# A conv block on one core: other places for every operation, and a depthwise chain whose taps are placed over 1.86 jobs instead of one

## The chip, the cores and the metric

The kernel runs on one core of one Trainium2 chip. The metric is the device time of one execution in microseconds (us). Five engines of the core matter: TensorE (PE in the profile, with its weight loads as PEld), VectorE (DVE), ScalarE (ACT), GpSimd (POOL) and SyncE (SP). Each works off its own list of instructions in the order in which the program holds them; an instruction that is not ready holds up everything behind it on its engine. SP and POOL also issue the DMA transfers.

## The reference

The input x has the shape (16, 128, 96, 96): 16 images, 128 channels, 96 rows of 96 pixels, all in float32. One layer is computed:

```python
x_hwc = x.transpose(0, 2, 3, 1)
xn1 = _layernorm(x_hwc, ln1_w, ln1_b)                      # over the 128 channels
x = x + _attention(xn1, wq, wk, wv, wp).transpose(0, 3, 1, 2)   # 8 heads, channels attend to channels
xn2 = _layernorm(x.transpose(0, 2, 3, 1), ln2_w, ln2_b).transpose(0, 3, 1, 2)
# _ffn, with HID = 512:
h1 = jnp.einsum('bchw,oc->bohw', xn2, w_in[:, :, 0, 0])    # 128 -> 512 channels
h2 = depthwise 3x3 conv of h1 with w_dw, padding 1          # 512 channels, each for itself
h3 = jax.nn.gelu(h2, approximate=False)
x = x + jnp.einsum('bchw,oc->bohw', h3, w_out[:, :, 0, 0])  # 512 -> 128 channels
```

The attention matrices are 16 x 16 per head, made from sums over all 9216 pixels of an image. So the first norm (called a) has to run over a whole image before its attention is known; then comes the second norm (b), band by band, and the feed-forward part behind it.

## The kernel before

Channels lie on the 128 partitions. An image is cut into 8 bands of 12 rows (`BR`), a band into 3 units of 4 rows (`UR`, 384 pixels). The 512 hidden channels are 4 chunks of 128. A **job** is one band of one chunk: the hidden product on TensorE (`hidden`, L906), its copy from PSUM into one of four h1 buffers, one for each chunk (`kept`, L911, ScalarE), the nine taps of the depthwise conv, and the gelu (L944, ScalarE). There are 451 jobs, and not 512, because for some bands (`by_pe`) the conv of the fourth chunk is done wholly on TensorE, with weights that hold the tap (`comp`, L990).

The nine taps of an ordinary job are shared out in this way. The weights are scaled so that the centre tap has the factor 1. Two taps (three in one kind of job) are made by ScalarE as whole products into `pr` buffers (`products`, L919); POOL issues DMA transfers that add them, one into another (`add_last`, pr<-pr) and the sum into h3 (`add_first`, h<-pr; both L940). The five or six taps that are left are the **chain** on VectorE: the first one (L924) reads two windows of h1 and writes h3, and each later one (L930) multiplies a window of h1 by a column and adds h3 to it, in place. So each instruction of a chain needs the result of the one before it in that chain. The gelu needs h3 after the chain and after `add_first`. After it `out` (L1017, TensorE) sums four chunks per unit, and `add` (L1024, VectorE) adds that to x; SP stores the band.

Norm a and norm b run through transposes on TensorE (`forth`, L614), statistics on VectorE (`stats`, L621), two small instructions on POOL for the reciprocal root (`variance` and `power`, L628 and L632), for norm b a tiny shift on VectorE (`shift`, L636), a scaling on ScalarE (L668 and L672), transposes back (`back`, L719) and a copy into the padded xn buffers (`place`, L723 and L725). While band after band of one image goes through norm b and the feed-forward part, norm a of the next image is spread between.

**What sets the order.** No order is written out by hand. Every operation is recorded in a plan with its engine, an assumed duration, what it reads and writes, and a *place*: a number counted in jobs. A constant of its kind, from the table `AT`, is added to the number of the job (kinds that end in `_0` hold for the first image):

```python
    def at(kind, place, i=1):
        return place + AT[kind if i else kind + "_0"]
...
        for k, t in enumerate(left):
            dve(t_dve(tap_size(t)), at("tap", j + STEP["tap"] * k), lambda t=t: tap(t), h1, h3, True)
```

`Plan.order` then goes through an assumed course of the work: whenever an engine is free, it takes, of the operations whose needs are met and whose buffers are free, the one with the lowest place. A place is thus no time but a priority, compared with others on the same engine alone; a result counts as there only some hundred nanoseconds after its operation. For VectorE this means that the next instruction of a chain isn't ready in the moment in which its predecessor ends (`own`, 120 ns in the plan), and an instruction of another kind or of another chain is taken first if one is ready. For the buffers `tr`, `h3`, `pr`, `xb` and `x1` the order of the places is binding too (`IN_TURN`). The program then holds the operations of every engine in the order of their assumed starts. `AT`, at L37, and `STEP`, at L47, are all that the change touches; its table takes one line more, so that every line behind it has a number higher by one in the changed kernel.

Of the kernel before, what the change touches and what calls it, by code (L numbers as in the profile page):

```python
# [34 lines left out]
X1_BUFS, XB_BUFS, PR_BUFS, H3_BUFS, ZT_BUFS = 2, 6, 5, 10, 3  # L35
IN_TURN = ("tr", "h3", "pr", "xb", "x1")
AT = dict(  # L37
    load_w=-20.2, weights=13.4, zeros=-68.05, load_a=-147.85, forth_a=-13.65, stats_a=-60.15, variance_a=574.05,
    power_a=353.05, scaled_a=35.3, gram=0.3, back_a=-44.8, place_a=177.6, attention=-146.15, mix=-16.25,
    residual=204, mixed=-47.8, add_x=-331.2, forth_b=-11.5, stats_b=-104.75, variance_b=68.55, power_b=-326.9,  # L40
    shift_b=-87.05, scaled_b=162.15, back_b=-5.95, place_b=38.15, halo=227.9, hidden=2.75, kept=-114.4,
    products=153.15, add_last=-10.05, tap=4.7, add_first=-147.85, gelu=241.95, conv=3.5, conv_gelu=5.8, out=7,
    add=-70.85, store=278.2, mix_0=-75.3, residual_0=369.55, mixed_0=-142.3, add_x_0=-398.7, gram_0=126.2,
    forth_a_0=-269.2, forth_b_0=-14.9, stats_a_0=-113.85, stats_b_0=-48.05, scaled_a_0=100.95, scaled_b_0=286.6,
    back_a_0=-115.65, back_b_0=-181.55, place_a_0=-352.8, place_b_0=-9.75, shift_b_0=-101.75, late=-3.55,
)
STEP = dict(scaled=0.3, hidden=0.1, products=0.5, tap=0.166, conv=1.6, conv_tap=0.03, out=0.8, out_part=0.05)  # L47
SLACK = 300
NORM1_END = 6.0
EARLY = 5  # L50
# [162 lines left out]
def tile_restormer_block(  # L213
# [148 lines left out]
    def at(kind, place, i=1):  # L362
        return place + AT[kind if i else kind + "_0"]
# [5 lines left out]
    def z_units(k, r0, r1):  # L369

        return [("z", k, u) for u in range((r0 + UR - 1) // UR - 1, (r1 - 2) // UR + 1)]


    def t_mm(n):
        return 2 * max(111, 0.849 * n)

    def t_dve(n):
        return 100 + 1.067 * n if n > 2 * UT else 67 + 1.05 * n

    def t_act(n, scalars=0):  # L380
        return 95 + 93 * scalars + 0.832 * n
# [4 lines left out]
    def pe(ns, p, f, r, w):  # L386
        op("PE", ns, p, f, r, w, ns + 200 + SLACK, ns)

    def dve(ns, p, f, r, w, two=False):
        op("DVE", ns, p, f, r, w, ns + 120 + SLACK, ns + 120, two=two)  # L390
# [7 lines left out]
    def act(ns, p, f, r, w):  # L398
        op("ACT", ns, p, f, r, w, ns + 150 + SLACK, ns + 150)
# [155 lines left out]
    def norm(i, second, place_of):  # L555
# [41 lines left out]
        def pixels(s, m):  # L597
# [99 lines left out]
            for h, (q, tr) in enumerate(zip(qs, trs)):  # L697
                zt, sh = zt_of(q), s + STEP["scaled"] * h
                if by_dve:
# [8 lines left out]
        def zt_of(q):  # L708
            return ("h3", ("zT", q // 2), q % 2) if i == 0 and not second else ("zT", (name, q))
# [176 lines left out]
    def conv_job(j, g, n):  # L886
# [30 lines left out]
        def product(t):  # L917
            to = d["pr", t] = prp.tile([P, BR, W], F32, tag="pr", name=f"pr_{g}_{n}_{t}")
            nc.scalar.activation(to, shifted(t), AF.Copy, scale=ratio[:, n, t : t + 1])  # L919

        def tap(t):
            h3 = h3_of(g, n)
            if t == left[0]:
                nc.vector.scalar_tensor_tensor(  # L924
                    h3, shifted(t), ratio[:, n, t : t + 1], shifted(UNIT), ALU.mult, ALU.add
                )
                return
            lo, hi, cut = inside(t, b * BR, BR)
            to = h3[:, lo:hi, cut]
            nc.vector.scalar_tensor_tensor(  # L930
                to, shifted(t)[:, lo:hi, cut], ratio[:, n, t : t + 1], to, ALU.mult, ALU.add
            )

        def tap_size(t):
            lo, hi, cut = inside(t, b * BR, BR)
            return BR * W if t == left[0] else (hi - lo) * (cut.stop - cut.start)
# [16 lines left out]
        for k, (r, e) in enumerate(chunks):  # L953
            ph = ("h", (jn, r))
            jk, zs = j + STEP["hidden"] * k, z_units(kz, r0 + r, r0 + e)
            to = h1[k + 1 : k + 2] if r > 1 else h1[:2]
            pe(t_mm((e - r) * W), at("hidden", jk), lambda r=r, e=e: hidden(r, e), [*zs, ("w", "in")], [ph])
            act(t_copy((e - r) * W), at("kept", jk), lambda r=r, e=e: kept(r, e), [ph], to)
        for k, t in enumerate(dma_taps):
            jk = j + STEP["products"] * k  # L960
            act(t_act(BR * W, 1), at("products", jk), lambda t=t: product(t), h1, [("pr", (jn, t))])
# [3 lines left out]
        for k, t in enumerate(left):  # L965
            dve(t_dve(tap_size(t)), at("tap", j + STEP["tap"] * k), lambda t=t: tap(t), h1, h3, True)
        if dma_taps:
# [7 lines left out]
    def by_matmuls(p, g, s):  # L975
# [9 lines left out]
        def product(t):  # L985
            if t == order[0]:
                d["pc"] = rows(bank((g, PE_CHUNK, s), UT))
            lo, hi, cut = inside(t, b * BR + s * UR, UR)
            dy, dx = divmod(t, 3)
            nc.tensor.matmul(  # L990
                d["pc"][:, lo:hi, cut], lhsT=comp[:, t, :], rhs=window(xn, r0 + dy, UR, dx)[:, lo:hi, cut],
                start=(t == order[0]), stop=(t == order[-1]),
            )

        def columns(t):
            lo, hi, cut = inside(t, b * BR + s * UR, UR)
            return (hi - lo) * (cut.stop - cut.start)
# [4 lines left out]
        for k, t in enumerate(order):  # L1002
            dy = t // 3
            zs = z_units(kz, r0 + dy, r0 + dy + UR)
            pe(t_mm(columns(t)), at("conv", p + STEP["conv_tap"] * k), lambda t=t: product(t), [*zs, ("w", "conv")], [pc])
        act(t_act(UT), at("conv_gelu", p), gelu, [pc], [("h3", (g, PE_CHUNK), s)])

    def ffn_out(p, g, s):
# [5 lines left out]
        def product(k, n):  # L1014
            if k == 0:
                d["po"] = bank(("out", g, s), UT)
            nc.tensor.matmul(  # L1017
                rows(d["po"]), lhsT=woutT[:, n, :], rhs=h3s[g, n][:, s * UR : (s + 1) * UR, :],
                start=(k == 0), stop=(k == NCH - 1),
            )  # L1020
# [9 lines left out]
        for k, n in enumerate(order):  # L1030
            pk = p + STEP["out_part"] * k
            pe(t_mm(UT), at("out", pk), lambda k=k, n=n: product(k, n), [("h3", (g, n), s), ("w", "out")], [po])
# [69 lines left out]
```

## Time and profile before

| what | value |
|---|---|
| median of 3 runs (lowest to highest) | 4140.04 us (4127.82 to 4140.15) |
| the profiled execution's own time | 4139.28 us |
| its span in the trace | 4137.5 us |
| granted TensorE clock, mean over the span | 0.997 |
| TensorE busy, share of the span | 4064.3 us, 98% |
| VectorE busy | 4048.7 us, 98% |
| ScalarE busy | 3674.7 us, 89% |
| POOL busy | 2538.1 us, 61% |
| VectorE's chain instructions (L924 and L930) | 451 + 2129, together 3524.7 us |
| DMA adds issued by POOL (L940) | 578 + 450 of 576 KB each |

A row of a group has the line, the engine, the operation, what is written and read, the shapes and the count; then the busy time of the whole group and the mean duration of one instruction; then how long the engine had been idle just before instructions of the group, and what ended most of that. On VectorE an instruction's record reaches a little into that of the next one, so the cost of an instruction is better read as the distance from its start to the next start.

### The profile page before, as it was taken

To read this page: it belongs to the slowest core of one execution; us is meant where nothing else is said; L and a number is where in the kernel's file an instruction comes from. 1 tells how busy PE (TensorE), PEld (TensorE's weight loads), DVE (VectorE), ACT (ScalarE), POOL (GpSimd) and SP (SyncE) were. 2 spreads that over 40 slices of the span, in tenths; PEclk is the share of its full clock that TensorE was granted. 3 is DMA by queue.
4 is the path that set the end of the run, shared out by engine and by line. 5 is a ranking of instruction groups with operands and counts; after the bars stand their busy time and mean duration, and the time that the engine had idled before them with its cause. 6 is when DMAs were issued, how large, how long until landed. Compare 5 with 4: busy or idle time off the path is not lost.

```text
span 4137.5 us, 52025 instructions
## 1 busy us (share of the span) xinstructions
PE 4064.3 (98%) x17217; PEld 2630.9 (64%) x17217; DVE 4048.7 (98%) x4706; ACT 3674.7 (89%) x6993; POOL 2538.1 (61%) x2357
## 2 busy tenths in 40 slices
PE   8999999999999999999999999999999999999999
PEld 6666666666666666666666666666666666666555
DVE  6999999999999999999999999999999999999998
ACT  5899989999889998999899989999889989999886
POOL 4657656566665757657566665666646666566442
PEclk9999999999999999999999999999999999999999
DMA  2999999999999999999999999999999999999998
GB/s 87 193 195 213 205 213 204 206 217 199 211 203 204 209 198 209 216 200 207 199 216 197 209 201 206 213 207 204 200 198 211 205 213 209 194 208 205 192 195 187
DMA packets 205372, 833.50 MB, mean 201 GB/s; under 512 B 23728, under 2 KB 25136, under 8 KB 205104
## 3 DMA queue, kind: packets, MB, share of 16 engines
q0 software_dynamic: 165600, 678.37, 84.6%
q1 hardware_dynamic: 38256, 151.73, 9.8%
q8 instruction: 136, 2.23, 0.2%
q14 instruction: 132, 1.08, 0.1%
q10 hardware_dynamic: 1248, 0.09, 0.0%
HBM read 148.26 MB, written 75.50 MB: 54 GB/s over the span
## 4 chain that ended last, share of the span: by engine, by line
PE 40%; DVE 10%; ACT 5%; DMA 3%; issue 2%; POOL 1%; POOLq 0%; ACTq 0%; DVEq 0%
PE h L990 11%; PE h L1017 10%; PE h L906 8%; DVE h L930 7%; PE g L682 2%; PE h L571 2%; DMA h<-pr 2%; DVE h L924 2%; PE pB_a L719 1%; ACT pr L919 1%; PE pT_b L614 1%; PE pT_a L614 1%; PE pB_b L719 1%; DMA pr<-pr 1%; ACT h L911 1%
## 5 line engine op out<-in xcount | busy, mean ns | idle before, releaser
L930 DVE SCALAR_TENSOR_TENSOR h<-h,ratio,h 128x1140 f32<-128x1140 f32 (+3 forms) x2129 | 2890.9, 1378 | 5.0
L919 ACT ACTIVATE pr<-h,ratio 128x1152 f32<-128x1152 f32 x1028 | 1337.2, 1307 | 98.7 <-DMA h<-pr 63.1
L990 PE MATMUL h<-xn,comp 128*128 128x380 f32 (+1 forms) x3294 | 1160.5, 483 | 3.6 <-ACT h L911 1.5
L1017 PE MATMUL h<-h,woutT 128*128 128x384 f32 x3072 | 1129.9, 487 | 11.4 <-ACT h L944 4.7
L906 PE MATMUL h<-xn,winT 128*128 128x384 f32 (+2 forms) x2706 | 1055.9, 494 | 8.0 <-ACT h L911 6.1
L940 POOL DMA_DIRECT2D pr<-pr x578 | 558.3, 977 | 478.3 <-ACT pr L919 312.0
L990 PEld LDWEIGHTS h<-xn,comp 128*128 128x128 f32 x3294 | 596.9, 190 | 348.8 <-issue 6.5
L911 ACT COPY h<-h 128x384 f32<-128x384 f32 (+2 forms) x1353 | 670.0, 525 | 142.0 <-PE h L906 110.8
L1017 PEld LDWEIGHTS h<-h,woutT 128*128 128x128 f32 x3072 | 555.7, 190 | 347.1 <-issue 25.0
L906 PEld LDWEIGHTS h<-xn,winT 128*128 128x128 f32 x2706 | 485.6, 190 | 302.4 <-issue 35.9
L940 POOL DMA_DIRECT2D h<-pr x450 | 447.6, 998 | 361.5 <-PE h L906 73.8
L924 DVE SCALAR_TENSOR_TENSOR h<-h,ratio 128x1152 f32<-128x1152 f32 x451 | 633.8, 1408 | 5.0 <-ACT h L911 2.8
L944 ACT ACTIVATE h<-h 128x1152 f32<-128x1152 f32 x453 | 549.4, 1216 | 14.9 <-DMA h<-pr 8.9
L632 POOL TENSOR_TENSOR rstd_a<-ve_a,mhalf 128x4 f32<-128x4 f32 x288 | 535.3, 1859 | 13.0 <-POOL ve_a L628 0.2
L628 POOL TENSOR_SCALAR ve_a<-st_a 128x4 f32<-128x4 f32 x288 | 347.3, 1206 | 286.9 <-DVE st_a L621 263.2
L632 POOL TENSOR_TENSOR rstd_b<-ve_b,mhalf 128x4 f32<-128x4 f32 x288 | 516.5, 1794 | 10.6
L672 ACT ACTIVATE zT<-pT_b,nb_b,rstd_b 128x128 f32<-128x128 f32 x1132 | 434.3, 494 | 47.4 <-DVE nb_b L636 40.6
L628 POOL TENSOR_SCALAR ve_b<-st_b 128x4 f32<-128x4 f32 x288 | 285.5, 996 | 301.9 <-DVE st_b L621 285.5
L668 ACT ACTIVATE zT<-pT_a,rstd_a 128x128 f32<-128x128 f32 x1080 | 320.3, 422 | 18.9 <-POOL rstd_a L632 17.7
L682 PEld LDWEIGHTS g<-zT 128*128 128x128 f32 x2304 | 295.1, 192 | 45.0 <-issue 4.4
L682 PE MATMUL g<-zT 128*128 128x129 f32 x2304 | 305.1, 275 | 0.0
L571 PE MATMUL h<-xn,mwT 128*128 128x384 f32 x768 | 287.1, 490 | 6.6 <-ACT h L911 3.2
(171 smaller groups left out, 3585.7 us busy)
## 6 DMA issues: line engine op xcount, KB each, us to landing
pr<-pr POOLq DMA_DIRECT2D x578, 576.0 KB, 7.5
h<-pr POOLq DMA_DIRECT2D x450, 576.0 KB, 7.7
x<-in_x_dram SPq DMA_DIRECT2D x128, 576.0 KB, 6.8
out_dram<-x SPq DMA_DIRECT2D x127, 576.0 KB, 6.3
x<-in_x_dram POOLq DMA_DIRECT2D x122, 576.0 KB, 7.2
out_dram<-x SPq DMA_DIRECT2D x3, 192.0 KB, 1.9
weights<-in_L_conv_w_in_dram SPq DMA_DIRECT2D x1, 256.0 KB, 2.9
weights<-in_L_conv_w_out_dram SPq DMA_DIRECT2D x1, 256.0 KB, 3.0
```

What stands on the lines that cost most here:

```text
L628: nc.gpsimd.tensor_scalar(ve, d["mv"][:, :, 2], 1.0 / C, EPS, ALU.mult, ALU.add)
L632: nc.gpsimd.tensor_tensor(rstd, d["ve"], mhalf, ALU.pow)
L682: nc.tensor.matmul(grams[i][:, : P + 1], lhsT=zt[:, :P], rhs=zt, start=(q == 0 and k == 0), stop=(q == NU * TPU // QT - 1 and k == QT - 1),)
L906: nc.tensor.matmul(rows(ph), lhsT=winT[:, n, :], rhs=window(xn, r0 + r, e - r, 1), start=True, stop=True)
L911: nc.scalar.copy(window(h1_, r, e - r, 1), rows(d.pop(("ph", r))))
L919: nc.scalar.activation(to, shifted(t), AF.Copy, scale=ratio[:, n, t : t + 1])
L924: nc.vector.scalar_tensor_tensor(h3, shifted(t), ratio[:, n, t : t + 1], shifted(UNIT), ALU.mult, ALU.add)
L930: nc.vector.scalar_tensor_tensor(to, shifted(t)[:, lo:hi, cut], ratio[:, n, t : t + 1], to, ALU.mult, ALU.add)
L940: nc.gpsimd.dma_start(out=to, in_=d["pr", t], accum_op=ALU.add)
L944: nc.scalar.activation(h3, h3, AF.Gelu)
L990: nc.tensor.matmul(d["pc"][:, lo:hi, cut], lhsT=comp[:, t, :], rhs=window(xn, r0 + dy, UR, dx)[:, lo:hi, cut], start=(t == order[0]), stop ...
L1017: nc.tensor.matmul(rows(d["po"]), lhsT=woutT[:, n, :], rhs=h3s[g, n][:, s * UR : (s + 1) * UR, :], start=(k == 0), stop=(k == NCH - 1),)
```

## The change

All 55 constants of `AT` get other values, and `STEP["tap"]` goes from 0.166 to 0.31. With six instructions in a chain the places of its first and its last instruction then lie 5 x 0.31 = 1.55 jobs apart instead of 0.83; with seven it would be 1.86 instead of 1.00. The first tap of a job is placed at j + 3.85 instead of j + 4.7. The operations, their shapes, their counts and the buffers stay as they are; only the order in which each engine and each queue has them becomes another one.

```diff
 AT = dict(
-    load_w=-20.2, weights=13.4, zeros=-68.05, load_a=-147.85, forth_a=-13.65, stats_a=-60.15, variance_a=574.05,
-    power_a=353.05, scaled_a=35.3, gram=0.3, back_a=-44.8, place_a=177.6, attention=-146.15, mix=-16.25,
-    residual=204, mixed=-47.8, add_x=-331.2, forth_b=-11.5, stats_b=-104.75, variance_b=68.55, power_b=-326.9,
-    shift_b=-87.05, scaled_b=162.15, back_b=-5.95, place_b=38.15, halo=227.9, hidden=2.75, kept=-114.4,
-    products=153.15, add_last=-10.05, tap=4.7, add_first=-147.85, gelu=241.95, conv=3.5, conv_gelu=5.8, out=7,
-    add=-70.85, store=278.2, mix_0=-75.3, residual_0=369.55, mixed_0=-142.3, add_x_0=-398.7, gram_0=126.2,
+    load_w=-109.65, weights=162.45, zeros=-128.6, load_a=-160.95, forth_a=-14.1, stats_a=-107.15,
+    variance_a=623.35, power_a=363.65, scaled_a=89.4, gram=0.5, back_a=-97.05, place_a=195.75,
+    attention=-166.05, mix=-94.6, residual=128.6, mixed=-43.7, add_x=-354.15, forth_b=-11.35, stats_b=-144.3,
+    variance_b=116.35, power_b=-307.2, shift_b=-92.35, scaled_b=167.8, back_b=-80.35, place_b=79.2, halo=265.2,
+    hidden=2.65, kept=0.15, products=112.5, add_last=-100, tap=3.85, add_first=-149.15, gelu=282.5, conv=3.6,
+    conv_gelu=4.45, out=6.65, add=-4.1, store=318.7, mix_0=-164.1, residual_0=380.6, mixed_0=-152.85,
...
 )
-STEP = dict(scaled=0.3, hidden=0.1, products=0.5, tap=0.166, conv=1.6, conv_tap=0.03, out=0.8, out_part=0.05)
+STEP = dict(scaled=0.3, hidden=0.1, products=0.5, tap=0.31, conv=1.6, conv_tap=0.03, out=0.8, out_part=0.05)
```

More of the change, by code (lines that the diff above doesn't have):

```diff
@@ L37 @@
 AT = dict(
-    load_w=-20.2, weights=13.4, zeros=-68.05, load_a=-147.85, forth_a=-13.65, stats_a=-60.15, variance_a=574.05,
-    power_a=353.05, scaled_a=35.3, gram=0.3, back_a=-44.8, place_a=177.6, attention=-146.15, mix=-16.25,
-    residual=204, mixed=-47.8, add_x=-331.2, forth_b=-11.5, stats_b=-104.75, variance_b=68.55, power_b=-326.9,
-    shift_b=-87.05, scaled_b=162.15, back_b=-5.95, place_b=38.15, halo=227.9, hidden=2.75, kept=-114.4,
-    products=153.15, add_last=-10.05, tap=4.7, add_first=-147.85, gelu=241.95, conv=3.5, conv_gelu=5.8, out=7,
-    add=-70.85, store=278.2, mix_0=-75.3, residual_0=369.55, mixed_0=-142.3, add_x_0=-398.7, gram_0=126.2,
-    forth_a_0=-269.2, forth_b_0=-14.9, stats_a_0=-113.85, stats_b_0=-48.05, scaled_a_0=100.95, scaled_b_0=286.6,
-    back_a_0=-115.65, back_b_0=-181.55, place_a_0=-352.8, place_b_0=-9.75, shift_b_0=-101.75, late=-3.55,
+    load_w=-109.65, weights=162.45, zeros=-128.6, load_a=-160.95, forth_a=-14.1, stats_a=-107.15,
[4 more added lines that the diff above has]
+    conv_gelu=4.45, out=6.65, add=-4.1, store=318.7, mix_0=-164.1, residual_0=380.6, mixed_0=-152.85,
+    add_x_0=-278.55, gram_0=309.25, forth_a_0=-319.05, forth_b_0=-13.45, stats_a_0=18.75, stats_b_0=-86.95,
+    scaled_a_0=-5, scaled_b_0=398.05, back_a_0=-169.75, back_b_0=-158.95, place_a_0=-451.8, place_b_0=0.85,
+    shift_b_0=-52.6, late=-3.85,
 )
-STEP = dict(scaled=0.3, hidden=0.1, products=0.5, tap=0.166, conv=1.6, conv_tap=0.03, out=0.8, out_part=0.05)
+STEP = dict(scaled=0.3, hidden=0.1, products=0.5, tap=0.31, conv=1.6, conv_tap=0.03, out=0.8, out_part=0.05)
 SLACK = 300
```

## The prediction

> **What bounds the kernel now.** I read the page first (busy shares, groups), then the busy time by stretches, then the waits, then VectorE's timeline. The page shows two engines that are both nearly full:
>
> ```profile
> PE 4064.3 (98%) x17217; PEld 2630.9 (64%) x17217; DVE 4048.7 (98%) x4706; ACT 3674.7 (89%) x6993; POOL 2538.1 (61%) x2357
> ...
> PE 40%; DVE 10%; ACT 5%; DMA 3%; issue 2%; POOL 1%; POOLq 0%; ACTq 0%; DVEq 0%
> ...
> L930 DVE SCALAR_TENSOR_TENSOR h<-h,ratio,h 128x1140 f32<-128x1140 f32 (+3 forms) x2129 | 2890.9, 1378 | 5.0
> ...
> L924 DVE SCALAR_TENSOR_TENSOR h<-h,ratio 128x1152 f32<-128x1152 f32 x451 | 633.8, 1408 | 5.0 <-ACT h L911 2.8
> ```
>
> The reader is to see that the chain of work passes from engine to engine, with no single owner, and that the chain instructions stand with only 5.0 + 5.0 us of idle time before them. The busy time by stretches (PE, PEld, DVE, ACT, POOL, then clock, DMA share, GB/s) tells where time is left:
>
> ```profile
> 100.00:200.00 100.00, 92.40 (x401) 60.00 (x400) 96.11 (x106) 89.15 (x173) 64.53 (x59) 0.97 0.92 195
> 200.00:800.00 600.00, 595.22 (x2533) 385.38 (x2532) 596.32 (x691) 549.57 (x1053) 385.04 (x345) 1.00 0.96 204
> 800.00:1600.00 800.00, 792.26 (x3392) 514.69 (x3391) 792.59 (x909) 726.60 (x1393) 509.80 (x460) 1.00 0.97 207
> 1600.00:2400.00 800.00, 790.66 (x3375) 512.17 (x3374) 791.22 (x906) 728.00 (x1393) 515.62 (x462) 1.00 0.97 206
> 2400.00:3200.00 800.00, 787.90 (x3337) 511.38 (x3337) 785.06 (x896) 720.16 (x1372) 505.43 (x453) 0.99 0.96 204
> 3200.00:4000.00 800.00, 787.48 (x3211) 499.26 (x3210) 792.49 (x892) 718.30 (x1340) 474.09 (x437) 1.00 0.97 204
> 4000.00:4138.00 138.00, 133.67 (x437) 78.96 (x435) 127.04 (x117) 92.16 (x146) 42.82 (x45) 0.99 0.87 184
> ```
>
> From 200 to 4000 us VectorE is idle for 3.7 + 7.4 + 8.8 + 14.9 + 7.5 = 42.3 us, TensorE for 4.8 + 7.7 + 9.3 + 12.1 + 12.5 = 46.4 us, and the DMA engines are busy at 0.96 to 0.97. An order that changes no instruction can only work on such idle time. The rest, about 47 us of VectorE's, lies in the start and the end. What VectorE waits for is short and scattered:
>
> ```profile
> DVE st_a L621 <- PE h L614: 13.7, 12, 5.3
> DVE x L1024 <- PE h L1017: 10.3, 11, 2.0
> DVE st_a L621 <- PE pT_a L614: 10.3, 7, 3.2
> DVE nb_b L636 <- POOL rstd_b L632: 9.9, 12, 2.2
> DVE st_b L621 <- PE pT_b L614: 7.8, 11, 2.1
> ```
>
> (us in total, times, the longest.) The first row is the start; the others are some 40 waits of about a microsecond.
>
> **What one link of a chain costs.** A second cost doesn't show as idle time. In the timeline of VectorE these instructions follow each other:
>
> ```profile
> 2047.67 1.40 DVE L924 SCALAR_TENSOR_TENSOR h<-h,ratio 128x1152 f32<-128x1152 f32 x1
> 2049.11 2.86 DVE L930 SCALAR_TENSOR_TENSOR h<-h,ratio,h 128x1140 f32<-128x1140 f32 x2
> 2051.89 1.41 DVE L924 SCALAR_TENSOR_TENSOR h<-h,ratio 128x1152 f32<-128x1152 f32 x1
> 2053.22 0.15 DVE L636 SCALAR_TENSOR_TENSOR nb_b<-st_b,rstd_b 128x4 f32<-128x4 f32 x1
> ```
>
> The first and the third are the same instruction. Behind the first stands the next of its own chain, and 1.44 us pass from start to start; behind the third stands something else, and 1.33 us pass. Over the whole trace the median distance of a 1152-wide chain instruction is 1444 ns with its own successor behind it (54 cases) and 1329 ns otherwise; of a 1140-wide one 1431 against 1316. So a link that isn't parted costs 115 ns. The program before has 140 of them among its 2129 links: 140 x 0.115 = 16.1 us.
>
> The Trainium skill, "VectorE: DVE Perf Modes", section "The DRAIN you can't avoid", says that chaining costs nothing extra: eight copies took the same time with a semaphore after each as with one at the end. By that rule no parting of chains is worth anything; the trace disagrees, with 1444 against 1329 ns.
>
> **The change, part by part.**
>
> *Chains run through each other.* I counted the order of instructions in both programs. Links with nothing between: 140 before, 141 after. Links with exactly one instruction between: 1039 before, 847 after. From the first to the last instruction of a chain lie 14.1 instructions of VectorE before and 14.5 after, in work 12.4 and 12.9 us; with 4137.5 / 451 = 9.2 us for a job that is 1.35 and 1.40 jobs. The chains of before already run through each other, since the plan takes another chain whenever a link isn't ready. The wider step is hardly to be seen in the result: +1 link x 0.115 = +0.1 us.
>
> *The order elsewhere.* To see what moves, I placed each instruction of the new order at the time at which its engine, in the profile of before, had done as much work as stands in front of it. Chain instructions move by -0.6 to +0.4 us on the mean. `products` stands 2.2 us earlier, the adds' issues on POOL 3 to 4 us earlier, the gelu 2.7 us, `out` 3.6 us and `add` 3.0 us earlier; norm b (`forth` to `place`) 4 to 6 us later, the conv on TensorE 2.3 us later; norm a and `hidden` stay within 1.3 us. Of the leads that this shortens, the largest is from `place` of norm b to `hidden`: its median goes from 42 to 35 us, its lowest twentieth from 15.3 to 7.7 us; still cover. If that cover were gone, `hidden` would stand still on TensorE, and behind it `out` and the conv. The gelu leads `out` by 23 us before and 22 after. I put both at 0. On SP the only early change is that one load goes ahead of the first store; loads land in 6.8 us by the page, and this is 0.
>
> *Start and end.* In front of the first chain instruction VectorE has 48.6 us of work before and 48.9 after, TensorE in front of the first `hidden` 65.0 and 68.3 us; the first `out` stands behind 119.9 and 113.8 us of TensorE's work. That is +0.3 us, with the rest covered by other work in front of it. At the end the last chain's last instruction is followed by five adds in both. 0.
>
> *Waits that an order makes by chance.* This is what can't be read off the counts. Every short wait of before goes, and others come. Its size is bounded on one side by the 42.3 us of idle time, all gone; on the other side by nothing but rows such as the waits on POOL (below). The nearest row for the usual case is the scatter of idle time between like stretches: per 800 us it is 4.9 (3.7 on 600), 7.4, 8.8, 14.9 and 7.5, with a standard deviation of 3.7. Over 3800 us that makes 3.7 x sqrt(4.75) = 8 us, and between two orders 8 x 1.41 = 11 us. I take 0 for the mean.
>
> *Sum.* 4139.28 (the profiled execution, 0.02% under the median of 4140.04) + 0.1 + 0.3 = 4139.7, which I round to **4139 us**.
>
> **The rivals.**
>
> *It is faster because waits thin out.* Speaking for it: `out` moves 0.6 us further ahead of `add`, and `forth` 0.6 us ahead of `stats`, two of the rows above. If 60% of the 42.3 us go, that is 4139 - 25 = 4114 us. Against it: nothing in the order's counts shows fewer meetings of an instruction with its supplier.
>
> *The chains really part.* If all 140 links were parted, 4139 - 16 = 4123 us. Against it stands the count of 141; only a link price that depends on what stands two places behind would bring it back, and the trace shows 1329 ns both for another chain and for other work as the follower.
>
> *It is slower because POOL's queue blocks norm b.* POOL issues the adds and does `variance` and `power` in one list. The issues move 3 to 4 us ahead, while the products they wait for move 2.2 us and the last link of a chain moves 0.4 us the other way. An issue that waits holds `power` behind it; then `shift` on VectorE is late, and all chain instructions behind it:
>
> ```profile
> POOL pr L940 <- ACT pr L919: 312.0, 177, 6.9
> ...
> ACT zT L672 <- DVE nb_b L636: 41.9, 47, 2.0
> ...
> POOL h L940 <- DVE h L930: 37.7, 17, 7.9
> ```
>
> VectorE now meets a late `power` 12 times in 288, at 9.9 / 12 = 0.83 us each. If it met it as often as ScalarE meets a late `shift`, 47 times, that would be 35 x 0.83 = +29 us: 4168 us. It decides from 15 further waits on (12.4 us). For it: the shifts above. Against it: `power` is ready 1.9 us ahead of `shift` in the median, and `shift` itself now comes 6 us later against 4 us for `power`.
>
> **How the numbers follow.** About 0.3%, 12.4 us here, is what a measurement of this kernel can tell from no change. The likeliest case, no change that can be told, has 0.42; by the 11 us of scatter alone it would be 0.74, but the five stretches come from one order, and another one can be better or worse as a whole. Thinner waits and parted chains together have 0.27 (0.03 of it the chains), the blocked POOL and other new waits 0.31. The likeliest case's own range is 4127 to 4151. For 8 in 10 the range goes down to 4106, where 33 of the 42 us are gone, and up to 4181, where 50 more waits of 0.83 us have come.
>
> **What would show it.** In the profile of the changed kernel I expect the same counts and mean durations for the chain (1378 and 1408 ns within 5), 141 unparted links at 115 ns, VectorE idle for 30 to 55 us between 200 and 4000 us, and a DMA share of 0.96 to 0.97. If POOL blocks, the row of nb_b waiting for rstd_b has 27 times or more and over 20 us. If the leads of norm b are too short, `hidden` waits for `place` (L723), a row that is missing now. The prediction is wrong if idle time on VectorE moves by more than 12 us either way, or if chain instructions change their durations because other neighbours, on POOL or in the DMA queues, meet them.

## The result, and the profile after

The changed kernel is a little slower: a ratio of 1.0022 to the kernel before, 95% interval 1.0013 to 1.0031 (medians 4145.57 and 4137.27 us, eight runs each). In a second comparison, beside the experiments, the ratio was 1.0009 (0.9999 to 1.0020; 4137.34 and 4131.36 us). By these ratios the change costs 9 us in the first comparison and 4 us in the second, whose interval reaches to no change at all. Both lie inside the 0.3% that the prediction counted as no change to be told, and on its slower side.

The page of the changed kernel, the lines that answer to those of before (its line numbers are higher by one):

```profile
PE 4064.7 (98%) x17217; PEld 2632.1 (63%) x17217; DVE 4051.5 (98%) x4706; ACT 3687.3 (89%) x6993; POOL 2482.2 (60%) x2357
...
PE 15%; DVE 15%; ACT 5%; DMA 2%; issue 1%; POOL 1%; DVEq 0%; ACTq 0%; POOLq 0%
...
L931 DVE SCALAR_TENSOR_TENSOR h<-h,ratio,h 128x1140 f32<-128x1140 f32 (+3 forms) x2129 | 2891.0, 1382 | 5.0
...
L925 DVE SCALAR_TENSOR_TENSOR h<-h,ratio 128x1152 f32<-128x1152 f32 x451 | 635.8, 1410 | 20.0 <-ACT h L912 14.3
```

TensorE is as busy as before to 0.4 us (4064.7 against 4064.3), VectorE to 2.8 us, while this execution's span is 4151.0 us, 13.5 more. So 10.7 of the 13.5 us are idle time of VectorE and not work. But this execution, at 4153.02 us, was the longest of the eight. One row stands out: the first instruction of a chain now has 20.0 us of idle time before it (5.0 before), mostly waits for ScalarE's copy of the hidden product. The busy time by stretches of the changed kernel (PE, PEld, DVE, ACT, POOL; clock, DMA share, GB/s):

```profile
200.00:800.00 600.00, 590.32 (x2506) 382.28 (x2505) 588.69 (x684) 546.45 (x1042) 382.86 (x344) 1.00 0.96 204
800.00:1600.00 800.00, 787.20 (x3337) 509.14 (x3336) 788.99 (x899) 722.58 (x1374) 490.70 (x454) 1.00 0.97 205
1600.00:2400.00 800.00, 788.57 (x3378) 513.81 (x3377) 790.67 (x904) 729.20 (x1394) 492.54 (x459) 1.00 0.98 207
2400.00:3200.00 800.00, 787.79 (x3345) 510.49 (x3344) 784.72 (x897) 722.92 (x1372) 495.87 (x456) 1.00 0.96 204
3200.00:4000.00 800.00, 787.85 (x3223) 500.02 (x3222) 790.14 (x891) 721.49 (x1354) 466.25 (x439) 1.00 0.96 202
```

VectorE is idle here for 11.3 + 11.0 + 9.3 + 15.3 + 9.9 = 56.8 us, 15 more than the 42.3 before. The first story that offers itself is thus: norm b stands 6 us later, the hidden product of a band's first job comes late, the copy too, and the first chain instruction waits. The experiments were made against this story.

### The profile page after: what moved, and what is told of

Read it like the earlier page. It is cut to its first block, busy times and chain, and to the rows that moved or that the text cites. A ratio compares the mean times of both kernels' runs of the same rounds, so it can differ in the third digit from the quotient of the medians.

```text
span 4151.0 us, 51952 instructions
## 1 busy us (share of the span) xinstructions
PE 4064.7 (98%) x17217; PEld 2632.1 (63%) x17217; DVE 4051.5 (98%) x4706; ACT 3687.3 (89%) x6993; POOL 2482.2 (60%) x2357
## 5 line engine op out<-in xcount | busy, mean ns | idle before, releaser
L931 DVE SCALAR_TENSOR_TENSOR h<-h,ratio,h 128x1140 f32<-128x1140 f32 (+3 forms) x2129 | 2891.0, 1382 | 5.0
L1018 PE MATMUL h<-h,woutT 128*128 128x384 f32 x3072 | 1117.5, 488 | 16.4 <-ACT h L912 10.8
L907 PE MATMUL h<-xn,winT 128*128 128x384 f32 (+2 forms) x2706 | 1034.8, 494 | 10.9 <-ACT h L912 6.1
L941 POOL DMA_DIRECT2D pr<-pr x578 | 549.8, 961 | 463.9 <-ACT pr L920 330.3
L941 POOL DMA_DIRECT2D h<-pr x450 | 426.0, 953 | 542.3 <-PE h L1018 71.3
L925 DVE SCALAR_TENSOR_TENSOR h<-h,ratio 128x1152 f32<-128x1152 f32 x451 | 635.8, 1410 | 20.0 <-ACT h L912 14.3
L633 POOL TENSOR_TENSOR rstd_a<-ve_a,mhalf 128x4 f32<-128x4 f32 x288 | 515.7, 1791 | 12.6 <-POOL ve_a L629 0.2
L629 POOL TENSOR_SCALAR ve_a<-st_a 128x4 f32<-128x4 f32 x288 | 292.9, 1017 | 249.1 <-DVE st_a L622 194.9
```

The lines of the kernel that those rows point to most:

```text
L629: nc.gpsimd.tensor_scalar(ve, d["mv"][:, :, 2], 1.0 / C, EPS, ALU.mult, ALU.add)
L633: nc.gpsimd.tensor_tensor(rstd, d["ve"], mhalf, ALU.pow)
L907: nc.tensor.matmul(rows(ph), lhsT=winT[:, n, :], rhs=window(xn, r0 + r, e - r, 1), start=True, stop=True)
L925: nc.vector.scalar_tensor_tensor(h3, shifted(t), ratio[:, n, t : t + 1], shifted(UNIT), ALU.mult, ALU.add)
L931: nc.vector.scalar_tensor_tensor(to, shifted(t)[:, lo:hi, cut], ratio[:, n, t : t + 1], to, ALU.mult, ALU.add)
L941: nc.gpsimd.dma_start(out=to, in_=d["pr", t], accum_op=ALU.add)
```

## The experiments

Three theories stood against each other. **N**: the late norm b makes the first chain instructions wait. **S**: the wider step itself makes them eager, so that they meet late copies. **R**: the table of before is finely balanced, and any step away from it costs. One more run measures the price of a link. All kernels compute the whole reference. A chain's "link" is an instruction that follows its own predecessor in the chain; it is "unparted" when nothing stands between the two on VectorE.

**The tap part by itself.**

```diff
 # on the kernel before
-STEP = dict(scaled=0.3, hidden=0.1, products=0.5, tap=0.166, ...)
+STEP = dict(scaled=0.3, hidden=0.1, products=0.5, tap=0.31, ...)
```

> The kernel before with STEP tap 0.31 alone and its own table of places (moving tap from 4.7 to 3.85 as well gives the identical order, so this is the tap part of the change by itself). Unparted links 197 instead of 140, links with one instruction between 815 instead of 1046. Theory N (late norm b makes first taps wait): norm b stays where it was, lead of its copy over the hidden product 9.9 us in the lowest twentieth (11.4 before), so idle time in front of first chain instructions stays near 5 us; time +57 x 0.115 = +6.6 us, about 4144. Theory S (the step itself makes the first taps eager, they meet late copies): idle in front of first chain instructions 15 us or more, time +15 to +20. Theory R (any other order costs): +8 us with waits of any kind.

Measured: 4158.1 against 4128.01 us, ratio 1.0070 (1.0056 to 1.0083), some 29 us slower. That is three times what the whole change costs. The step didn't part the chains, it left 57 more links unparted; at 118 ns each in this trace they make 6.7 us, and some 22 us are left for new waits. The profile shows a part of them: VectorE is idle for 51.9 us between 200 and 4000 us, 10 to 13 more than in the two profiles of the kernel before (42.3, and 39.1 in the second one below). The waits in front of first chain instructions stay far under S's 15 us. VectorE's waits in this kernel (us in total, times, the longest):

```profile
DVE x L1024 <- PE h L1017: 18.1, 20, 3.0
...
DVE st_a L621 <- PE pT_a L614: 10.4, 9, 2.6
...
DVE h L924 <- ACT h L911: 5.9, 7, 2.3
```

Here it is `add` that waits for `out`, 20 times instead of 11. N's +6.6 us is far too little; S, with 15 to 20 us, comes nearest in size but has the wrong place; new waits "of any kind", as R has it, fit, though they cost more than the 8 us that R gave.

**Norm b put back in the changed kernel.**

```diff
 # on the changed kernel
-    ... forth_b=-11.35, ...
+    ... forth_b=-13.0, ...
```

> The changed kernel with forth_b at -13.0 instead of -11.35: norm b stands 8 us earlier again, its lead over the hidden product 13.2 us in the lowest twentieth (5.2 in the changed kernel, 11.4 before). Unparted links 173 (141). Theory N: idle in front of first chain instructions falls from 20 us to 5 to 8 us; time against the changed kernel -13 + 32 x 0.115 = -9 us, so level with the kernel before or 1 us over it. Theory S: it stays at 15 us or more and the time is +4 us over the changed kernel, some 12 us over the kernel before. Theory R: 5 to 12 us over the kernel before, waits spread over all rows.

Measured: 4138.54 against 4128.01 us, ratio 1.0025 (1.0015 to 1.0035). That is what the changed kernel has, 1.0009 to 1.0022, and not level with the kernel before. First chain instructions still wait for copies:

```profile
DVE h L925 <- ACT h L912: 9.3, 13, 1.9
...
DVE h L925 <- PE h L1018: 6.3, 9, 1.5
```

N said 5 to 8 us of idle time here and a gain; neither came.

**Norm b made late in the kernel before.**

```diff
 # on the kernel before
-    ... forth_b=-11.5, ...
+    ... forth_b=-10.0, ...
```

> The kernel before with forth_b at -10.0 instead of -11.5: norm b 8 us later, its lead over the hidden product 4.6 us in the lowest twentieth, as in the changed kernel, with the chain step left at 0.166. Unparted links 115 (140 before), -2.9 us. Theory N: idle in front of first chain instructions rises from 5 to 15 us or more, and the time by 7 us or more net. Theory S: that idle time stays near 5 us and the time falls by about 3 us. Theory R: up by about 8 us with waits elsewhere.

Measured: 4152.93 against 4128.01 us, ratio 1.0057 (1.0044 to 1.0070): 24 us slower with 25 fewer unparted links. The time rose as N said, but hardly by N's way, as the waits show:

```profile
DVE st_b L621 <- PE pT_b L614: 18.6, 12, 3.7
...
DVE h L924 <- ACT h L911: 6.9, 10, 1.3
```

The statistics of norm b wait for their transposes (18.6 us; 7.8 before), the shift waits 13.0 us for `power` (9.9 before), and the first chain instructions wait little. That the wider step is all that costs is refuted here (S said 3 us faster). R's direction holds again.

**The price of a link.**

```diff
 # on the kernel before, in the plan's helper for VectorE
-        op("DVE", ns, p, f, r, w, ns + 120 + SLACK, ns + 120, two=two)
+        op("DVE", ns, p, f, r, w, ns + 120 + SLACK, ns, two=two)
```

> The kernel before, planned with no delay between two links of a chain on VectorE: the chains run one after another, 1330 unparted links instead of 140. This measures the price of a link in the whole. If an unparted link costs 115 ns and VectorE is the bound, +1190 x 0.115 = +137 us, about 4275 us. If the distance only shows in the records and something else sets the end, under +40 us.

Measured: 4273.57 against 4128.01 us, ratio 1.0349 (1.0335 to 1.0363): +146 us for 1190 more unparted links, 122 ns for each, new waits included. In VectorE's timeline four instructions of one chain, with nothing between them, take 5.64 us from the first start to the start behind them:

```profile
2009.93 5.73 DVE L930 SCALAR_TENSOR_TENSOR h<-h,ratio,h 128x1152 f32<-128x1152 f32 x4
2015.57 0.16 DVE L636 SCALAR_TENSOR_TENSOR nb_b<-st_b,rstd_b 128x4 f32<-128x4 f32 x1
```

In the kernel before, four instructions of two chains that take turns need 5.26 us:

```profile
2038.44 5.35 DVE L930 SCALAR_TENSOR_TENSOR h<-h,ratio,h 128x1140 f32<-128x1140 f32 x4
2043.70 0.42 DVE L621 BATCH_NORM_STATS2 st_b<-pT_b 128x6 f32<-128x256 f32 x1
```

Of the 0.38 us between them 0.01 is for one tile of 1152 instead of 1140, and the rest is three unparted links. The page agrees, with VectorE busy for 4156.8 us, 108 more than before (the rest of a link's price is a gap of some 36 ns in front of the next instruction, which counts as idle), and every link's own excess over the parted distance is 116 ns in this trace:

```profile
PE 4110.6 (96%) x17217; PEld 2620.5 (61%) x17217; DVE 4156.8 (97%) x4706; ACT 3687.0 (86%) x6993; POOL 2493.1 (58%) x2357
```

So the price that the prediction read from 54 cases holds for the whole, and VectorE is a bound: what is added to its list comes out at the end nearly one to one.

**Both kernels once more.** No edit; the changed kernel beside the following experiments, and the kernel before once more.

> The changed kernel once more, beside the others of this group. All theories: 0.1 to 0.3% over the kernel before, as in the first comparison. A second profile shows how far its single waits repeat.

> The kernel before once more, for a second profile: how much of its idle time on VectorE (42.3 us between 200 and 4000 us) repeats, and which waits. Expected within 5 us of 42.

Measured: ratio 1.0009 (0.9999 to 1.0020) for the changed kernel; 4135.12 us for the kernel before in its profiled run. The second profile of the changed kernel, its waits on VectorE:

```profile
DVE x L1025 <- PE h L1018: 9.6, 11, 2.0
DVE h L925 <- ACT h L912: 9.1, 9, 2.3
DVE nb_b L637 <- POOL rstd_b L633: 4.3, 6, 1.2
```

The row that stood out is 9.1 us instead of 14.3. The sums of the five stretches from 200 to 4000 us, of the changed kernel and then of the kernel before:

```profile
sum 3800.00, PE 3757.75 PEld 2427.03 DVE 3764.02 ACT 3456.28 POOL 2304.43; mean PE 751.55 PEld 485.41 DVE 752.80 ACT 691.26 POOL 460.89
```

```profile
sum 3800.00, PE 3756.34 PEld 2422.66 DVE 3760.94 ACT 3445.20 POOL 2362.66; mean PE 751.27 PEld 484.53 DVE 752.19 ACT 689.04 POOL 472.53
```

VectorE's idle time between 200 and 4000 us is 36.0 us in this execution, against 56.8 in the first one of the very same program; the kernel before had 42.3 and 39.1. One execution's idle time thus moves by 20 us with no edit at all, and two single profiles can't carry a difference of 15. The first story rested on this. In this second pair of profiles the changed kernel's execution is even the shorter one, 4132.2 against 4133.3 us of span.

**A trifle moved in the kernel before.**

```diff
 # on the kernel before
-    ... hidden=2.75, ...
+    ... hidden=2.7, ...
```

> The kernel before with one place moved by a trifle: hidden 2.70 instead of 2.75. Kinds move by 2 us at most, norm b keeps its lead (11.1 against 11.4 us in the lowest twentieth), but the fine order is another one: 186 unparted links instead of 140. Theory R (the table of before is finely balanced and any step away from it costs, wherever it goes): +46 x 0.115 = 5 us for the links and 5 to 15 us of new waits, in all +10 to +20 us. Theories S and N (it needs the wider step or a late norm b): +5 us, links alone.

Measured: 4147.06 against 4131.36 us, ratio 1.0042 (1.0028 to 1.0057): 17 us slower, where the links alone explain 46 x 0.118 = 5.4 us. The time lies in R's 10 to 20 us, but R's new waits show only in part. In this profile VectorE is idle for 41.1 us between 200 and 4000 us, no more than in the kernel before; over the whole span it is idle for 92.1 us, 8 more than in the kernel before's second profile, and more than half of that comes after 4000 us. Where the rest of the 12 us beyond the links went is not shown. An edit of a twentieth of a job, with no step widened and no norm moved, costs more than the whole change.

**The tap part undone in the changed kernel.**

```diff
 # on the changed kernel
-    ... tap=3.85, ...   and   tap=0.31 in STEP
+    ... tap=4.7, ...    and   tap=0.166 in STEP
```

> The changed kernel with the tap part undone (tap 4.7, STEP tap 0.166), all other new places kept. Unparted links 115 (141). Theory S (the wider step costs): faster than the changed kernel by 10 us or more, level with the kernel before. Theory R (the new places were balanced for the wider step, and a change of the step by itself costs, in this direction too): slower than the changed kernel, by 10 us or more, with new waits on VectorE although 26 fewer links are unparted.

Measured: 4189.21 against 4131.36 us, ratio 1.0134 (1.0118 to 1.0150). With both old tap constants in the new table the kernel is 55 us slower than before and some 50 us slower than the changed one, with 115 unparted links, as few as in any order so far. S said level with the kernel before. The waits on VectorE, and the first row of the page:

```profile
DVE st_b L622 <- PE pT_b L615: 25.0, 26, 6.0
DVE st_a L622 <- PE pT_a L615: 21.7, 19, 2.9
DVE x L1025 <- PE h L1018: 14.6, 18, 2.8
```

```profile
PE 4085.6 (98%) x17217; PEld 2639.3 (63%) x17217; DVE 4053.3 (97%) x4706; ACT 3687.1 (88%) x6993; POOL 2442.1 (58%) x2357
```

A part that no theory named shows on TensorE: its granted clock is 0.993 on the mean of these five runs against 0.997 in the kernel before beside them, and the same 17217 matmuls are busy for 4085.6 us instead of 4064.3. How much of the 55 us this makes is not shown.

So the tap part costs 29 us when it is brought into the old table and 50 us when it is taken out of the new one: its worth depends on the other 54 constants. Which of the part's two constants counts in the new table is not shown, since this run moved both, the step and the tap's place. The plan's assumed end (explained with the next runs) points to the place: with the step narrowed and the tap left at 3.85 it is 4119.9 us, near the changed kernel's 4117.4, and with the tap at 4.7 as well it is 4157.7. No run took the two apart, so the step's width is neither shown to be the cause nor cleared.

**Two further searches.** The plan goes through an assumed course of the work, and the end of that course can be had from the kernel's own code, before any run. A random search kept edits of places and steps that lower it; in the first kernel steps were free (the search made the tap step 0.103), in the second the tap step stayed at 0.31. Almost all constants change, so only some are shown.

```diff
 # on the kernel before
-    ... variance_a=574.05, power_a=353.05, products=153.15, add_last=-10.05, tap=4.7, add_first=-147.85, ...
-STEP = dict(... products=0.5, tap=0.166, ... conv_tap=0.03, ...)
+    ... variance_a=606.5, power_a=528.42, products=47.22, add_last=1.65, tap=4.99, add_first=-247.61, ...
+STEP = dict(... products=0.4912, tap=0.1031, ... conv_tap=0.036, ...)
...
 # on the changed kernel
-    ... forth_a=-14.1, hidden=2.65, back_a=-97.05, mixed=-43.7, tap=3.85, conv_gelu=4.45, ...
+    ... forth_a=-14.28, hidden=2.62, back_a=-386.38, mixed=-249.35, tap=3.61, conv_gelu=3.93, ...
```

> The kernel before after a further random search over its places and steps, which kept what lowers the end of the plan's own assumed course (4108.7 us before, 4103.7 now; the search took STEP tap down to 0.103). Unparted links 126 (140). Theory B (balance: the time of an order follows the plan's assumed end, plus the scatter of single executions): -5 us, ratio 0.9988. Theory 'the assumed end is of no use below 10 us': no difference, ratio 0.999 to 1.001 or any sign.

> The changed kernel after the same kind of search with STEP tap held at 0.31 (assumed end 4117.4 for the changed kernel, 4112.6 now). Unparted links 112 (141). Theory B: +4 us over the kernel before, 5 us under the changed kernel. Theory S (a wider step costs by itself whatever the places): still 10 us or more over the kernel before.

Measured: the first has a ratio of 0.9973 (0.9963 to 0.9982), 4120.49 against 4133.80 us. It is faster than both kernels, by some 11 us against the one before, so R as worded, that any step away from the old table costs, is too strong. Its stretches on VectorE show where:

```profile
800.00:1600.00 800.00, 792.86 (x3388) 514.75 (x3387) 795.98 (x912) 732.10 (x1402) 515.25 (x461) 1.00 0.98 208
1600.00:2400.00 800.00, 794.23 (x3401) 516.40 (x3400) 795.22 (x911) 734.12 (x1400) 512.33 (x464) 1.00 0.98 209
...
3200.00:4000.00 800.00, 788.43 (x3206) 500.80 (x3205) 796.30 (x891) 719.82 (x1339) 469.68 (x435) 1.00 0.97 204
sum 3800.00, PE 3764.17 PEld 2430.85 DVE 3774.39 ACT 3462.83 POOL 2391.81; mean PE 752.83 PEld 486.17 DVE 754.88 ACT 692.57 POOL 478.36
```

Over all five stretches the idle time is 25.6 us, against 42.3 and 39.1 in the two profiles of the kernel before; the 126 unparted links give another 1.6 us. The second has 1.0019 (1.0010 to 1.0028), 4141.18 us: with 29 fewer unparted links than the changed kernel and a lower assumed end it isn't measurably better than that one's 1.0009 to 1.0022. Theory B hit the first by its sign (and gained twice the 5 us); for the second it said +4 us, which is the edge of the measured interval of 4 to 12 us. S's 10 us or more lies in that interval too, so this run doesn't rule S out.

All orders side by side; the assumed end is the plan's own, worked out from each kernel's own code, as a difference to the 4108.7 us of the kernel before. The last column follows from the ratio, in its last row from the medians:

| kernel | unparted links | assumed end, us | measured ratio (95%) | in us |
|---|---|---|---|---|
| before | 140 | 0 | 1 | 0 |
| the change, first and again | 141 | +8.7 | 1.0022 (1.0013 to 1.0031), 1.0009 (0.9999 to 1.0020) | +9, +4 |
| tap part by itself | 197 | +21.2 | 1.0070 (1.0056 to 1.0083) | +29 |
| changed, norm b put back | 173 | +17.8 | 1.0025 (1.0015 to 1.0035) | +10 |
| before, norm b late | 115 | +25.8 | 1.0057 (1.0044 to 1.0070) | +24 |
| before, hidden at 2.7 | 186 | +12.9 | 1.0042 (1.0028 to 1.0057) | +17 |
| changed, tap part undone | 115 | +49.0 | 1.0134 (1.0118 to 1.0150) | +55 |
| searched from before | 126 | -5.0 | 0.9973 (0.9963 to 0.9982) | -11 |
| searched, step 0.31 | 112 | +3.9 | 1.0019 (1.0010 to 1.0028) | +8 |
| links costing nothing in the plan | 1330 | +3.0 | 1.0349 (1.0335 to 1.0363) | +146 |

Unparted links alone explain nothing but the last row. The assumed end gives the others within 8 us, though only for the two searches was it forecast before the run; it fails in the last row, since there it was told that a link costs nothing.

## Why the prediction was right and wrong

*The likeliest case* was no change that can be told, at 4139 us, with its own range to 4151. The medians came out at 4145.57 and 4137.34 us, by the ratios 9 and 4 us over the kernel before. The size was right within the bound; but the first comparison puts the change clear of zero, on the slower side, and the sum held nothing for it: its terms are +0.1 and +0.3 us. (The sum of 4139.7 us also rounds to 4140 and not to 4139, which turned a forecast of +0.4 us into one just below the time of before.)

*The link's price* was right. Read as 115 ns from start distances, it came out as 118 ns in the changed kernel's trace, 116 ns in the run with 1330 of them, and 122 ns by that run's time. The rule of the Trainium skill that was cited beside it ("VectorE: DVE Perf Modes", "The DRAIN you can't avoid") speaks of a semaphore after each of eight copies and does not say that each copy read the one before. Taken as a rule for these chains, as the prediction took it, it would have had the last row of the table at +0; it is +146 us, waits included. For chains of this kind, each instruction reading what the one before it wrote, the measurement decides.

*That the chains don't part* was right: 141 unparted links cost 16.7 us in the changed kernel's trace, against 16.2 us before. The rival of really parted chains didn't occur. The 1.86 jobs of the title hold for no chain here: of the 451 chains 322 have six instructions, 128 have five and the last one has eight, so the usual span of the places is 1.55 jobs instead of 0.83.

*The step that failed* is "I take 0 for the mean" for the waits that an order makes by chance. It treated the order of before as one draw among equal ones. In its place the runs showed +4 to +9 us for the change itself, and that an order reached by a small edit is usually worse: three edits of the old table were slower by 17, 24 and 29 us, and of two edits of the new table one was slower by 50 us and one level. As far as these five edits and one search that won 11 us show, both tables lie near a low point, and the old one not at it. What the change brought was a loss of 29 us from the tap part and a regain of 20 to 25 us by the other 54 constants; taken in the other order, a loss of 55 us from those constants and a regain of some 50 us by the tap part. The prediction saw neither of the two, and that their small difference fell within its 12 us is luck. A figure for this term could be had beforehand from the kernel's own code: the plan's assumed end is 8.7 us later for the changed kernel, though such figures were off by up to 8 us in the table above. Why each part costs what it does is shown only in part, by the rows of waits above. The second mistake in the same step is the scatter of 11 us, taken from five stretches of one execution as a property of orders: the idle time differs by more than that between two executions of the same program (56.8 and 36.0 us).

*The leads* were put at 0, norm b's among them. In the changed kernel no wait of the hidden product for `place` shows among the waits of TensorE, as predicted. Putting norm b back brought no time, but making it late in the old table cost 24 us, and there the largest new waits are those of its statistics and shift, not of the hidden product. So "still cover" was right for the place that it named, and the changed kernel's loss isn't shown to come from norm b.

*The rival of POOL's blocked queue* didn't occur. The shift on VectorE waited for `power` 12 times for 9.1 us in the first profile and 6 times for 4.3 us in the second (12 times for 9.9 us before).

*What the profile was to show*: durations of 1382 and 1410 ns (within 5 of 1378 and 1408), a DMA share of 0.96 to 0.98 and, for VectorE's idle time, 57 and 36 us where 30 to 55 was said. By the prediction's own sign, idle time moving by more than 12 us, the first profile speaks against it (14.5 us more) and the second doesn't (6.3 us less).

*What stays open*: which wait of the changed kernel makes its 4 to 9 us. The waits for the copy in front of first chain instructions are the largest new row in both of its profiles (14.3 and 9.1 us; 2.8 and 4.2 us in the two of before), so they are the best candidate; but the one edit that aimed at them left them at 9.3 us, and no run took them away alone.

## What to carry to other kernels

Where three resources are 96 to 98% full and a search has set the order, judge an edit of one or two constants by re-balancing the others or not at all: by itself it cost 17 to 50 us here in four cases of five, and what it would be worth with the others re-balanced can't be seen from that. If the kernel carries a planner, its own figure for the new order sorted these orders better than counts of neighbours did, as long as each delay that the chip shows (here 115 ns for a link) is in it. And before a wait in one profile is called the cause, take a second profile of the same program.

## What the runs showed of the hardware

An instruction on VectorE that reads what the instruction right before it wrote starts 116 to 121 ns later than one that doesn't, by the mean of each trace, for tiles of 128 x 1045 to 128 x 1152 in float32. In the trace of the kernel before, with tiles of 128 x 1140, a statistics instruction between the two (0.34 us from start to start) hides all of it: 1648 ns for the two together with the own chain behind them (244 cases), 1649 with another one (126). The small shift (0.07 us) hides about half: 1440 ns (8 cases) against 1389 (54). Over 1190 such links the kernel is 3.5% longer, new waits included.

Idle time of one program differed by 20 us between two of its executions (the changed kernel's VectorE between 200 and 4000 us: 56.8 and 36.0), while its busy time stays within 2.2 us (4051.5 and 4049.3).
